# Cross attention: the value projection of an encoder chunk, taken apart from its key projection

## Chip, cores and metric

The kernel runs on one core of a Trainium2 chip. The metric is the device time of one execution in microseconds; the time before is the median of 7 runs. One further execution was profiled.

## What is computed

A post-norm decoder layer on `x` of 16 batches of 100 tokens, width 512: causal self-attention (16 heads of 32), cross attention to 361 encoder tokens per batch, and a mixture of 8 experts of which two are taken. Each of the three is added to its input and layer-normalised. The change lies in cross attention, in fp32:

```
q = rmsnorm((x @ Wq + bq) by 16 heads of 128) * qn_w
k = rmsnorm((enc @ Wk + bk) by 4 heads of 128) * kn_w     # each k, v head serves 4 q heads
v = (enc @ Wv + bv) by 4 heads of 128
out = softmax(q k^T / sqrt(128) + mask) v                 # per batch and head: 100 x 361 scores
x = layernorm(x + out @ Wo)
```

## The kernel before

**Products in three parts.** An fp32 operand is split into a high and a low half: `split` copies the high half (L137, mostly on ScalarE, a CAST in the profile) and subtracts it (L140, on VectorE, or on GpSimd where the source is not in PSUM). `mm3` then issues three matmuls, high by high (L145), low by high (L146), high by low (L147). `mmk` does so for four blocks of 128 of the contraction, so a projection of one chunk of tokens is 12 matmuls of 512 columns.

**Stages.** Self-attention comes first, then the q projections of all tokens (`b_q`), then cross attention, then the output projection (`d_part`), routing, the experts and the last norm. Queries go to memory (`qd`) and come back per batch and head group; attention outputs go to memory (`od`) and come back per tile of 128 tokens.

**Cross attention by units.** A unit is one batch `b` and one group `g` of four query heads that share a key and value head, so there are 64 units, four to a batch. The 361 encoder tokens of a batch are cut into three chunks (`CH`: 128, 128 and 105). The loop over `order` does, in each unit:

- for the next batch: `fetch_ctx` and `split_ctx` (encoder tokens, turned, tile `cT`, two buffers for three chunks), `kv_project`, and `kv_turn` one unit later;
- `x_load` of the queries for the unit after the next (`qf`, L732), which are split into the weight buffers WH and WL;
- the steps of `("s0", "a-", "t0", "s1", "s2", "t1", "a0", "t2", "s3", "a1")`: `s` is `x_scores` of one head of the next unit, `t` is `x_turn` of one chunk of this unit, `a` is `x_attend` of one chunk, where `a-` is the last chunk of the unit before;
- in every third unit from the ninth on, one row of `Wo` (`load_row`: a load of 256 KB on the sync queue at L480, tile `f_wo`, then a split into WH and WL by ScalarE and GpSimd). There are 16 such rows.

`kv_project` makes the keys of a chunk (`pk`), adds the bias (`ks`, L697, VectorE), makes its values (`pv`) and splits them into a slot of WH and WL, and then takes the RMS norm of the keys: four sums of squares (`ksq`, L706, VectorE), `rms_scale` and `rsqrt` (`v_k`, then `a_k` and `y_k` on ScalarE, then `t_k` and `r_k` on VectorE), and a product on GpSimd (L717). `kv_turn` transposes the normed keys (`ptk`, L727) and splits them (`kT`).

`x_scores` makes scores `s` of 100 x 362, adds the mask and takes the extreme in one VectorE instruction (L746), the exponential with its sum on ScalarE (L757), a reciprocal (L758), and the scaling on GpSimd (L759). `x_turn` transposes the probabilities of a chunk, one transpose per head (`ptp`, L767), and splits them (`pT`). `x_attend` adds the chunk's product to `av`, and after the last chunk ScalarE writes `o` (L787), which is stored to `od` (L792).

**Who sets the order.** The program is written in the order above, and a scheduler with a timeline model of its own then orders each engine's instructions; so a projection may stand some units ahead of its place in the source. Some loads are kept in program order on the sync queue. PSUM has 8 banks, two for each of the tags `mm` (projections), `s`, `t` (transposes) and `av`; keys and values of all chunks share the two of `mm`. Engines run their instructions in the built order, each waiting on semaphores.

Of the kernel before, what the change touches and what calls it, by code (L numbers as in the profile page):

```python
# [17 lines left out]
B, S, D = 16, 100, 512  # L18
# [8 lines left out]
CH = [(0, 128), (128, 128), (256, SE - 256)]  # L27
# [35 lines left out]
def tile_decoder_layer(  # L63
# [42 lines left out]
    def bank(tag, shape, name):  # L106
        return ps[-1].tile(shape, FP, name=name, tag=tag)
# [4 lines left out]
    def pair(p, shape, name, tag=None, bufs=None):  # L112
        k = {} if bufs is None else {"bufs": bufs}
        tag = tag or name
        return Pair(
            p.tile(shape, FR, name=f"{name}_h", tag=f"{tag}_h", **k),
            p.tile(shape, FR, name=f"{name}_l", tag=f"{tag}_l", **k),
        )
# [14 lines left out]
    def split(dst, src, high=None, low=None):  # L133

        high, low = high or nc.scalar, low or nc.vector
        if high is nc.scalar:
            ins = nc.scalar.copy(dst.h, src)  # L137
        else:
            ins = high.tensor_copy(dst.h, src)  # L139
        low.tensor_tensor(dst.l, src, dst.h.bitcast(FP), ALU.subtract)  # L140
        return ins

    def mm3(out, a, b, start, stop):

        nc.tensor.matmul(out, a.h, b.h, start=start, stop=False)  # L145
        nc.tensor.matmul(out, a.h, b.l, start=False, stop=False)  # L146
        nc.tensor.matmul(out, a.l, b.h, start=False, stop=stop)  # L147

    def mmk(out, a, b, n=KC):
        for k in range(n):  # L150
            mm3(out, a(k), b(k), k == 0, k == n - 1)
# [31 lines left out]
    def rms_scale(ss, p, n, name, p_=None):  # L183
        v = (p_ or small).tile([128, n], FP, name=f"v_{name}", tag=f"rms_v{n}")
        nc.vector.tensor_scalar(v[:p], ss, 1.0 / HD2, EPS_RMS, ALU.mult, ALU.add)
        return rsqrt(v[:p], p, n, name, p_=p_)
# [9 lines left out]
    def slot_of(s):  # L196
        return Pair(WH[:, s], WL[:, s])
# [324 lines left out]
    for k in range(KC):  # L522
        i = 4 * NU - 8 + k
# [113 lines left out]
    CT = {}  # L637

    def fetch_ctx(b):
        CT[b] = kvp.tile([128, KC, SE], FP, name=f"cf_{b}", tag="cf")  # L640
        nc.sync.dma_start(CT[b], ctxT[b])

    def split_ctx(b, i):
        c0, n = CH[i]
        CT[b, i] = pair(kvp, [128, KC, 128], f"cT_{b}_{i}", tag="cT", bufs=2)
        split(CT[b, i][:, :, :n], CT[b][:, :, c0 : c0 + n], low=nc.gpsimd)
# [34 lines left out]
    VS, KS, QX = {}, {}, {}  # L681
    wk, wv = units["wk"], units["wv"]

    spare = [slot_of(s)[:, k] for s in (4, 5) for k in range(KC)]

    def kv_project(b, i):
        c0, n = CH[i]
        if i == 0:
            K[b] = pair(w2, [128, NKV, SP], f"kT_{b}", tag="kT")
            nc.gpsimd.memset(K[b].h[:, :, SE:].bitcast(FP), 0.0)  # L690
            nc.gpsimd.memset(K[b].l[:, :, SE:].bitcast(FP), 0.0)
        ct = CT.pop((b, i))
        m = b * len(CH) + i
        pk = bank("mm", [128, D], f"pk2_{b}_{i}")
        mmk(pk[:n], lambda k: ct[:, k, :n], lambda k: wk[:, k, :])
        ks = w0.tile([128, D], FP, name=f"ks_{b}_{i}", tag="ks")
        nc.vector.tensor_tensor(ks[:n], pk[:n], bk_bc[:n], ALU.add)  # L697
        pv = bank("mm", [128, D], f"pv2_{b}_{i}")
        mmk(pv[:n], lambda k: ct[:, k, :n], lambda k: wv[:, k, :])
        VS[b, i] = spare[m % 6]  # L700
        split(VS[b, i][:n], pv[:n])
        kr = ks[:n].rearrange("p (h d) -> p h d", d=HD2)
        ss = small.tile([128, NKV], FP, name=f"kss_{b}_{i}", tag="kss")
        sq = w0.tile([128, HD2], FP, name=f"ksq_{b}_{i}", tag="sq", bufs=1)
        for h in range(NKV):
            nc.vector.tensor_tensor_reduce(  # L706
                out=sq[:n],
                in0=kr[:, h, :],
                in1=kr[:, h, :],
                scale=1.0,  # L710
                scalar=0.0,
                op0=ALU.mult,
                op1=ALU.add,
                accum_out=ss[:n, h : h + 1],
            )
        rs = rms_scale(ss[:n], n, NKV, f"k_{b}_{i}")
        nc.gpsimd.tensor_tensor(  # L717
            kr, kr, rs[:n].unsqueeze(2).to_broadcast([n, NKV, HD2]), ALU.mult
        )
        KS[b, i] = kr  # L720

    def kv_turn(b, i):
        c0, n = CH[i]
        kr = KS.pop((b, i))
        pt = bank("t", [128, NKV, 128], f"ptk_{b}_{i}")
        for h in range(NKV):
            nc.tensor.transpose(pt[:, h, :n], kr[:, h, :], ident[:n, :n])  # L727
        split(K[b][:, :, c0 : c0 + n], pt[:, :, :n])

    def x_load(b, g):  # L730
        qf = w0.tile([128, GR, S], FP, name=f"qf_{b}_{g}", tag="qf")
        nc.sync.dma_start(qf, qd[b][:, g * GR : (g + 1) * GR, :])  # L732
        QX[b, g] = spare[6 + g % 2][:, : GR * S].rearrange("p (h s) -> p h s", s=S)
        split(QX[b, g], qf, low=nc.gpsimd)
# [63 lines left out]
    for i in range(len(CH)):  # L798
        if i == 2:
            split_ctx(0, 2)  # L800
        kv_project(0, i)
        kv_turn(0, i)
    x_load(0, 1)
    for h in range(GR):
# [4 lines left out]
    def d_open():  # L809
        kv_l.close()  # L810
        inp["d"] = pool(d_i, "d_in", 2)
# [5 lines left out]
    def d_load(i):  # L817
        t, g = parts[i]
        n = TT[t][1]
        p = inp["d"]  # L820
        of = p.tile([128, GR, 128], FP, name=f"of_{t}_{g}", tag="of")
        nc.sync.dma_start(of[:, :, :n], od[t][:, g * GR : (g + 1) * GR, :n])
        OT[t, g] = pair(p, [128, GR, 128], f"ot_{t}_{g}", tag="ot")
        split(OT[t, g][:, :, :n], of[:, :, :n], low=nc.vector if i % 2 else nc.gpsimd)

    def d_part(i, among={}):

        t, g = parts[i]
        n = TT[t][1]
        if g == 0:  # L830

            tag = "av" if t == NT - 1 else "s" if t in (3, 4) else "mm"
            X1[t] = bank(tag, [128, D], f"acc_{t}")
        o, w = OT.pop((t, g)), units[f"wo_{g}"]
        for h in range(GR):
            mm3(
                X1[t][:n],
                o[:, h, :n],
                w[:, h, :],
                g == h == 0,  # L840
                g == NKV - 1 and h == GR - 1,
            )
            if h in among:
                among[h]()

    def d_norm(t):
        t0, n = TT[t]
        acc = X1.pop(t)
        p = w3 if t >= HEAD else inp["d"]
        x2 = p.tile([128, D], FP, name=f"x1_{t}", tag="x1", bufs=1 if t < HEAD else 3)  # L850
        nc.sync.dma_start(x2[:n], x1d[t][:n])
        nc.vector.tensor_tensor(x2[:n], acc[:n], x2[:n], ALU.add)
        layernorm(x2[:n], x2[:n], n, f"ln2_{t}")
        nc.sync.dma_start(x2d[t0 : t0 + n, :], x2[:n])
        X2[t] = x2
# [6 lines left out]
    for i, (b, g) in enumerate(order):  # L862
        if b == B - 1:
            if g == 0:
                d_open()
                d_load(0)
            for j in range(HEAD * g, HEAD * (g + 1)):
                d_load(j + 1)
                d_part(j)
                if parts[j][1] == NKV - 1:  # L870
                    d_norm(parts[j][0])
        if b + 1 < B:
            if g == 0:
                fetch_ctx(b + 1)
                split_ctx(b + 1, 0)
            if g < len(CH):
                kv_project(b + 1, g)
            if g + 1 < len(CH):
                split_ctx(b + 1, g + 1)
        if i + 2 < len(order):  # L880
            x_load(*order[i + 2])
        if b + 1 < B and g == NKV - 1:
            kv_turn(b + 1, 2)
        if b + 1 < B and 1 <= g < NKV - 1:
            kv_turn(b + 1, g - 1)
        nxt = order[i + 1] if i + 1 < len(order) else None
        for what in ("s0", "a-", "t0", "s1", "s2", "t1", "a0", "t2", "s3", "a1"):
            if what[0] == "s":
                if nxt:
                    x_scores(*nxt, int(what[1]))  # L890
            elif what[0] == "t":
                x_turn(b, g, int(what[1]))
            elif what[1] != "-":
                x_attend(b, g, int(what[1]))
            elif i:
                x_attend(*order[i - 1], 2)
        if i % 3 == 2 and 8 <= i < 8 + 3 * NKV * KC:
            w, k = divmod((i - 8) // 3, KC)
            load_row(f"wo_{w}", wo_slot[w], Wo4[w], k)
# [451 lines left out]
    for i in range(HEAD * NKV, len(parts)):  # L1351
        t, g = parts[i]
# [477 lines left out]
```

## Time and profile before

| what | value |
|---|---|
| median of 7 runs | 1409.3 us (1406.37 to 1413.98) |
| profiled execution | 1411.19 us |
| its span, first to last instruction | 1409.4 us |
| mean granted TensorE clock | 0.976 |
| cross attention, from the first scores to the last value projection | about 440 to 990 us |
| TensorE, VectorE, ScalarE, GpSimd busy (share of the span) | 95%, 67%, 54%, 50% |

In the profile PE is TensorE's matmuls, PEld its weight loads, DVE VectorE, ACT ScalarE, POOL GpSimd, SP or SPq the queue that issues most DMAs. A row of a timeline gives the start and the duration in us, the engine, the source line, the operation, the tile written and the tiles read, shapes, a count, and in brackets the idle time before it with what ended it. Matmuls are pipelined: one starts before the one before it has ended, so distances between starts are what counts. A mean granted clock under 1 means that the throttle held TensorE at half speed for stretches.

### The profile page before, as it was taken

The numbers are of one execution on the slowest core, as the hardware profiler recorded it, in microseconds if no ns is written. First come the engines' busy times: TensorE is split into PE (matmuls) and PEld (weight loads), VectorE is DVE, ScalarE is ACT, GpSimd is POOL, SyncE is SP. The second block draws the span as 40 slices with busy tenths as digits, with TensorE's granted clock in tenths as the row PEclk, the third lists the DMA queues.
The fourth block names the chain that finished last, engine by engine and source line by source line (L and its number), as shares of the span: only waits on it lengthen the run. The fifth ranks groups of instructions, "written<-read, shape, count | busy, mean of one in ns | idle before, by whom it ended". The sixth has DMA issues, their size and how long they took to land.

```text
span 1409.4 us, 25131 instructions
## 1 busy us (share of the span) xinstructions
PE 1337.6 (95%) x7952; PEld 1109.6 (79%) x7952; DVE 939.6 (67%) x2932; ACT 757.4 (54%) x1899; POOL 711.7 (50%) x839
## 2 busy tenths in 40 slices
PE   8999989999999999999999999999999898899895
PEld 7888868888878888888888888888887675677773
DVE  5766576766467777777777667767653558854577
ACT  4666653444446666666666656656663233333356
POOL 6877663344245555556555545555455345542530
PEclk9999999999999999999999999999999899899997
DMA  5221244645442122333233222322436545667883
GB/s 160 73 94 49 63 146 127 144 91 117 101 94 71 43 70 71 74 80 71 70 76 76 65 56 64 76 70 49 123 97 189 170 166 165 185 223 255 255 250 118
DMA packets 197872, 159.79 MB, mean 113 GB/s; under 512 B 133322, under 2 KB 152878, under 8 KB 197742
## 3 DMA queue, kind: packets, MB, share of 16 engines
q1 hardware_dynamic: 187904, 137.83, 35.8%
q0 software_dynamic: 4576, 14.95, 3.4%
q10 hardware_dynamic: 5262, 5.41, 1.3%
q8 instruction: 65, 1.06, 0.3%
q14 instruction: 65, 0.53, 0.1%
HBM read 107.16 MB, written 50.99 MB: 112 GB/s over the span
## 4 chain that ended last, share of the span: by engine, by line
PE 71%; DVE 13%; DMA 7%; ACT 4%; issue 3%; SPq 1%; POOL 1%; ACTq 0%; DVEq 0%; POOLq 0%
PE pq L145 4%; PE pq L147 4%; PE pq L146 4%; PE pv L145 4%; PE pv L146 4%; PE pv L147 4%; PE ptp L767 3%; PE pk L145 3%; PE pk L147 3%; PE pk L146 3%; PE s L145 3%; PE s L147 3%; PE s L146 3%; PE av L146 2%; DMA f_e<-in_expert_w 2%
## 5 line engine op out<-in xcount | busy, mean ns | idle before, releaser
L759 POOL TENSOR_SCALAR p<-p,sums 100x361 f32<-100x361 f32 x256 | 146.5, 577 | 101.5 <-DVE sums L758 90.5
L746 DVE CUSTOM_DVE_ANT_0 p<-s,nmask 100x361 f32<-100x361 f32 x256 | 133.0, 527 | 63.5 <-PE s L147 54.7
L757 ACT ACTIVATE p<-p,nm 100x361 f32<-100x361 f32 x256 | 153.2, 601 | 40.3 <-DVE nm L746 37.0
L140 DVE TENSOR_TENSOR pT_l<-ptp,pT_h 128x400 fp32r<-128x400 f32 (+1 forms) x192 | 107.5, 567 | 56.0 <-ACT pT_h L137 55.5
L145 PE MATMUL pq<-WH 128*128 128x512 f32 (+2 forms) x272 | 106.7, 392 | 5.5 <-DVE WH L139 5.5
L767 PE MATMUL ptp<-ident,p 100*128 100x100 f32 (+1 forms) x768 | 107.6, 252 | 0.0
L137 ACT CAST pT_h<-ptp 128x400 fp32r<-128x400 f32 (+1 forms) x192 | 91.2, 487 | 29.9 <-PE ptp L767 29.5
L140 POOL TENSOR_TENSOR cT_l<-cf,cT_h 128x512 fp32r<-128x512 f32 (+1 forms) x48 | 54.3, 1133 | 103.3 <-ACT cT_h L137 101.3
L767 PEld LDWEIGHTS ptp<-ident,p 100*128 100x128 f32 (+1 forms) x768 | 95.7, 152 | 13.4 <-POOL p L759 2.3
L146 PE MATMUL pq<-WL,WH 128*128 128x512 f32 (+2 forms) x272 | 104.0, 382 | 0.0
L147 PE MATMUL pq<-WH,WL 128*128 128x512 f32 (+2 forms) x272 | 103.8, 382 | 0.0
L147 PE MATMUL acc<-WH,ot_l 128*128 128x512 f32 (+1 forms) x208 | 86.6, 417 | 7.8 <-DVE ot_l L140 6.2
L145 PE MATMUL acc<-WH,ot_h 128*128 128x512 f32 (+1 forms) x208 | 86.2, 415 | 5.5 <-ACT ot_h L137 5.5
L145 PE MATMUL s<-kT_h,WH 128*100 128x362 f32 x256 | 88.2, 355 | 0.6 <-ACT kT_h L137 0.6
L145 PE MATMUL av<-pT_h,WH 128*128 128x400 f32 (+1 forms) x192 | 76.7, 400 | 8.5 <-ACT pT_h L137 8.1
L146 PE MATMUL acc<-WL,ot_h 128*128 128x512 f32 (+1 forms) x208 | 84.7, 407 | 0.0
L147 PE MATMUL s<-kT_h,WL 128*100 128x362 f32 x256 | 84.5, 330 | 0.0
L146 PE MATMUL s<-kT_l,WH 128*100 128x362 f32 x256 | 83.9, 328 | 0.0
L614 POOL TENSOR_TENSOR qs<-qs,r_q 128x512 f32<-128x512 f32 (+1 forms) x52 | 54.0, 1068 | 58.3 <-DVE r_q L169 47.9
L140 POOL TENSOR_TENSOR WL<-qf,WH 128x400 fp32r<-128x400 f32 x64 | 67.3, 1053 | 30.1 <-ACT WH L137 26.5
L145 PE MATMUL pv<-WH,cT_h 128*128 128x512 f32 (+1 forms) x192 | 79.2, 412 | 0.9 <-DVE WL L140 0.9
L145 PE MATMUL pk<-WH,cT_h 128*128 128x512 f32 (+1 forms) x192 | 77.6, 404 | 0.2
(337 smaller groups left out, 4010.2 us busy)
## 6 DMA issues: line engine op xcount, KB each, us to landing
qf<-qd SPq DMA_DIRECT2D x64, 200.0 KB
of<-od SPq DMA_DIRECT2D x48, 256.0 KB
cf<-in_ctxT SPq DMA_DIRECT2D x16, 722.0 KB
eb<-in_expert_b SPq DMA_DIRECT2D x32, 256.0 KB
ysd<-h SPq DMA_DIRECT2D x32, 256.0 KB
f_e<-in_expert_w SPq DMA_DIRECT2D x30, 256.0 KB
f_wq<-in_Wq SPq DMA_DIRECT2D x16, 256.0 KB
f_wo<-in_Wo SPq DMA_DIRECT2D x16, 256.0 KB
```

What stands on the lines that cost most here:

```text
L137: ins = nc.scalar.copy(dst.h, src)
L140: low.tensor_tensor(dst.l, src, dst.h.bitcast(FP), ALU.subtract)
L145: nc.tensor.matmul(out, a.h, b.h, start=start, stop=False)
L146: nc.tensor.matmul(out, a.h, b.l, start=False, stop=False)
L147: nc.tensor.matmul(out, a.l, b.h, start=False, stop=stop)
L614: nc.gpsimd.tensor_tensor(qr[:, hs, :], qr[:, hs, :], rs[:n, hs].unsqueeze(2).to_broadcast([n, GR, HD2]), ALU.mult,)
L746: nc.vector.tensor_tensor_reduce(out=p, in0=sc[:, :SE], in1=nmask, scale=1.0, scalar=BIG, op0=ALU.add, op1=ALU.min, accum_out=nm,)
L757: nc.scalar.activation(p, p, AF.Exp, bias=nm, scale=-1.0, accum_out=sh)
L759: nc.gpsimd.tensor_scalar(p, p, sh, 1.0, ALU.mult, ALU.mult)
L767: nc.tensor.transpose(pt[:n, h, :], probs[h][:, c0 : c0 + n], ident[:S, :S])
```

## The change

`kv_project` is cut into `k_project` and `v_project`. The bodies are the same lines; the values of a chunk are no longer made between the bias and the norm of its keys. In the first batch both are called in turn. In the loop, a unit's keys stay where they were (units 0, 1 and 2), and the values of the three chunks are made in units 0, 2 and 3. So a unit has 24, 12, 24 and 12 projection matmuls where it had 24, 24, 24 and none, counted in the source. A chunk's encoder tokens (`CT[b, i]`) are now released by `v_project`.

```diff
-    def kv_project(b, i):
+    def k_project(b, i):
         c0, n = CH[i]
...
-        ct = CT.pop((b, i))
-        m = b * len(CH) + i
+        ct = CT[b, i]
         pk = bank("mm", [128, D], f"pk2_{b}_{i}")
         mmk(pk[:n], lambda k: ct[:, k, :n], lambda k: wk[:, k, :])
         ks = w0.tile([128, D], FP, name=f"ks_{b}_{i}", tag="ks")
         nc.vector.tensor_tensor(ks[:n], pk[:n], bk_bc[:n], ALU.add)
-        pv = bank("mm", [128, D], f"pv2_{b}_{i}")
-        mmk(pv[:n], lambda k: ct[:, k, :n], lambda k: wv[:, k, :])
-        VS[b, i] = spare[m % 6]
-        split(VS[b, i][:n], pv[:n])
         kr = ks[:n].rearrange("p (h d) -> p h d", d=HD2)
...
         KS[b, i] = kr
+
+    def v_project(b, i):
+        n = CH[i][1]
+        ct = CT.pop((b, i))
+        pv = bank("mm", [128, D], f"pv2_{b}_{i}")
+        mmk(pv[:n], lambda k: ct[:, k, :n], lambda k: wv[:, k, :])
+        VS[b, i] = spare[(b * len(CH) + i) % 6]
+        split(VS[b, i][:n], pv[:n])
...
-        kv_project(0, i)
+        k_project(0, i)
+        v_project(0, i)
...
             if g < len(CH):
-                kv_project(b + 1, g)
+                k_project(b + 1, g)
+            for j in ((0,), (), (1,), (2,))[g]:
+                v_project(b + 1, j)
             if g + 1 < len(CH):
                 split_ctx(b + 1, g + 1)
```

## The prediction

> **What bounds the kernel now.** I read four things in this order: the page, the stage table cut into one encoder batch per row, the list of waits of TensorE for 400 to 990 us, and then timelines of single batches.
>
> ```profile
> span 1409.4 us, 25131 instructions
> PE 1337.6 (95%) x7952; PEld 1109.6 (79%) x7952; DVE 939.6 (67%) x2932; ACT 757.4 (54%) x1899; POOL 711.7 (50%) x839
> ...
> PE 71%; DVE 13%; DMA 7%; ACT 4%; issue 3%; SPq 1%; POOL 1%; ACTq 0%; DVEq 0%; POOLq 0%
> ```
>
> TensorE is busy 95% of the span and carries 71% of the chain that ended last. The change lies between about 434 and 990 us, so I ask how full TensorE is there. Two neighbouring batches, cut from one group of key sums to the next:
>
> ```profile
> 572.20:611.60 39.40, 38.75 (x218) 32.73 (x217) 28.80 (x110) 25.74 (x71) 22.44 (x31) 1.00 0.31 69
> 611.60:649.70 38.10, 37.86 (x217) 32.31 (x217) 27.71 (x110) 25.03 (x69) 21.03 (x30) 1.00 0.31 81
> ```
>
> After the window and its length come TensorE, weight loads, VectorE, ScalarE and GpSimd, each busy us and instructions, then the granted clock. A batch takes 38.1 to 39.4 us, of which TensorE is busy all but 0.2 to 0.7. No other engine passes 29. So there is no empty fourth unit: the scheduler already runs the projections some units ahead of their place in the source. Only waits can be won or lost, and the waits of TensorE name them:
>
> ```profile
> PE av L145 <- ACT pT_h L137: 8.1, 10, 1.7
> PE av L146 <- DVE pT_l L140: 4.2, 20, 0.5
> PE pv L145 <- DVE WL L140: 0.9, 1, 0.9
> PE s L145 <- ACT kT_h L137: 0.6, 2, 0.3
> ```
>
> Each row gives the sum, the count and the longest. Together they are 13.8 us in 15 batches, nearly all on turned probabilities (pT). Most of the 8.1 us has a DMA behind it. ScalarE works in order, and a cast of a Wo row stands in its queue before the row has landed:
>
> ```profile
> 629.01 0.59 ACT L787 ACTIVATE o<-av,bvT 128x400 f32<-128x400 f32 x1 [2.03 <-PE av L147]
> ...
> 632.94 0.64 ACT L137 CAST cT_h<-cf 128x512 fp32r<-128x512 f32 x1
> 634.78 0.62 ACT L137 CAST WH<-f_wo 128x512 fp32r<-128x512 f32 x1 [1.20 <-DMA f_wo<-in_Wo]
> 635.31 0.58 ACT L137 CAST WH<-pv 105x512 fp32r<-105x512 f32 x1
> ```
>
> The sync queue issues the row's load only after the store of o (L792 before L480), so the cast can start 634.78 - 629.01 = 5.8 us after o starts, whatever else happens. All 16 Wo rows wait like this, 24.6 us of ScalarE in sum. Whether TensorE pays depends on what stands behind the cast.
>
> **The change part by part.** Both programs have the same instructions (each TensorE, VectorE, ScalarE and GpSimd count is equal), so nothing is saved by itself; only order and buffers move. The sync queue's order is the same up to the last batch but for one swapped query load. From the built orders, one steady batch reads, with k1, k2, v1, v2 for the 12 products of a key or value chunk of the next batch, k0', v0' for the batch after, s for the three products of a head's scores, t for single transposes:
>
> before: ... [v1] ... [k2] s, t, s, t t, v2 in three pieces with t t between them, s, s, 6 products, ..., [k0'] ...
> after: ... [k2] ... [v1] s, t, s, six t, s, [v2] s, 1, s, 2, ..., [k0'] ...
>
> So k2 and v1 change places, and v2 goes whole behind the transposes. I price each place by distances in TensorE's row against the chain that must end in between. Steps of TensorE: 0.23 us per projection product, 0.16 to 0.18 per score or attend product, 0.09 per transpose.
>
> ```profile
> 513.86 0.40 PE L147 MATMUL pv<-WH,cT_l 128*105 128x512 f32 x1
> 514.09 0.40 PE L145 MATMUL pv<-WH,cT_h 128*105 128x512 f32 x1
> 514.33 0.34 PE L767 MATMUL ptp<-ident,p 100*128 100x100 f32 x2
> 514.44 0.46 PE L146 MATMUL pv<-WL,cT_h 128*105 128x512 f32 x1
> 514.74 0.39 PE L147 MATMUL pv<-WH,cT_l 128*105 128x512 f32 x1
> ```
>
> 1. v2 in one piece: after a pair of transposes the next product but one starts 0.30 us on (514.44 to 514.74) where 0.23 is usual (513.86 to 514.09). Two such breaks fewer in a batch, 14 batches: 2 x 0.07 x 14 = -2.0; new breaks of v0' and of head products by scores give some back. I take -1.4, between -2.6 and 0.
>
> 2. PSUM bank of v1 and v2. In the built program k2's bank is held until the ks evacuation (which waits for the k0 transposes, as before), so v2 takes v1's bank and waits for both splits of v1 (CAST WH, then TENSOR_TENSOR WL). Count from the start of v1's last product. ScalarE: cT_h of the next batch at 0.2 (it waits for v1, its buffer's last reader), WH at 0.7 to 1.3. VectorE first has the masked minimum of the score product behind v1 (1.0 to 1.5, from 0.48 us wait and 0.54 duration at 511.87), then WL 0.69, to 2.2. Behind the waiting cT_h on ScalarE stand WH of v1, o of unit 3 and an exponential, none due sooner. TensorE has in between: 0.23 + 0.5 + 0.36 + 0.09 + 0.5 + 0.53 + 0.5 = 2.7. Slack 0.5, price 0. The cover is those scores and transposes; without it 1 us per batch would show.
>
> 3. k0' behind v2 (it takes v2's bank). TensorE reaches it at 8.8 on the same count: 2.7, then 2.8 for v2, then s, 1, s, 2, four t, 3, the four key transposes, s: 0.5 + 0.18 + 0.5 + 0.36 + 0.36 + 0.55 + 0.4 + 0.5 = 3.3. Without a Wo row WL of v2 ends at 7.4: free. With one: in the new ScalarE order the row of Wo that is loaded after o of unit 3 stands ahead of cT_h and WH of v2 (before: the order is mixed, and k0' comes later behind v2). o starts at 1.3 at best, behind cT_h and WH of v1. The row lands at 1.3 + 5.8 = 7.1; casts at 7.1, 7.6, 8.1 (0.53 apart, as at 634.78 and 635.31), WH ends 8.7, WL 9.5. TensorE waits 0.7 in 4 batches (the rows return every third batch): 2.8.
>
> 4. The Wo row loaded after o of unit 0 (4 batches). Before, o stood ahead of the root of the key norm (a_k, y_k) on ScalarE; now behind a_k, a query cast and y_k, which wait for VectorE's sums:
>
> ```profile
> 601.54 0.60 ACT L787 ACTIVATE o<-av,bvT 128x400 f32<-128x400 f32 x1 [1.19 <-PE av L147]
> 602.03 0.20 ACT L157 ACTIVATE a_k<-v_k 105x4 f32<-105x4 f32 x1
> ...
> 607.40 0.62 ACT L137 CAST WH<-f_wo 128x512 fp32r<-128x512 f32 x1 [1.63 <-DMA f_wo<-in_Wo]
> ...
> 608.38 0.49 ACT L137 CAST pT_h<-ptp 105x400 fp32r<-105x400 f32 x1
> ```
>
> Walking VectorE's new order on from term 3 (WL, minimum, pT_l, ks, minimum, four key sums with kT_l among them) ends v_k at 12.2; a_k, cast and y_k then let o start at 13.3, which is 4.5 after k0'. Before it was 601.54 - 597.99 = 3.55. So the row lands 0.9 later, and the cast of the third chunk of pT stands behind it. TensorE, which comes 0.2 us later than before, waits 0.25 for pT_h and 0.46 for pT_l; it waited 0.25 to 0.4 before. Net 0.4 x 4 = 1.6.
>
> Walks 3 and 4 start every operation at once. Where the trace has such a tight run (second chunk of unit 2, at 536 us) the products came another 0.37 and 0.43 late. So I do not take the bare 0.7 and 0.4 but 0.9 and 0.8: 3.6 and 3.2. Ends: 0 (the load lands sooner) and 1.3 and 1.7 (o a little later), that is 0 to 12.
>
> Here a rule is weighed. "DMA: Bandwidth & Descriptors", section on the anatomy of one DMA, fits 2.0 us plus bytes by 436 GB/s for one DMA issued by GpSimd, a path that no run here times. That makes an estimate of 2.6 us for 256 KB, against 4.7 us from issue to cast here (630.05 to 634.78). By the rule both rows would have landed before ScalarE asks for them, and terms 3 and 4 would be nil. The rows of this kernel, 16 of 16 waited for, speak otherwise, and the sum goes by them.
>
> 5. Unit 2 (pT_l of the second chunk, 0.4 to 0.5 in nearly every batch) has the same instructions in the same order on TensorE, VectorE and ScalarE before and after: 0.
>
> 6. The last batch and the experts behind it: the scheduler also shuffles products of the output projection and, late, the turn and product of one expert slice. After 985 us TensorE is busy 378 of 425 us by the stage table, so order can matter there in both directions, and no row prices this one: 0, from -5 to +5.
>
> Sum: -1.4 + 3.6 + 3.2 = +5.4. The profiled execution took 1411.2 us (span 1409.4 and 1.8 around it), 1.9 above the median 1409.3. So 1416.6 for a like execution, 1414.7 against the median. About 0.3%, 4.2 us, is what a measurement of this kernel can tell from no change; the forecast is a little above it.
>
> **The rivals.** *Same* (0.30): the new waits are paid back. Whenever TensorE stands, ScalarE and VectorE catch up, and the 12.3 us of waits on pT (8.1 + 4.2) shrink by as much. For it: these waits are of the same kind. Against: they are short chains inside one unit that start from a TensorE product, so they do not profit from an earlier stop. Time 1409 to 1413. *Faster* (0.22): v1 behind k2 keeps its split out of VectorE's way before the reciprocals of heads 2 and 3 (sums at 509.71 stood behind WL at 509.11), everything behind it on VectorE comes 0.7 us sooner, and the waits on pT close. Half of them plus term 1 at its full size: -6 - 2 = -8, 1401. Against: TensorE did not wait at those reciprocals. *Much slower* (0.10, a part of slower): term 2's slack is lost. It needs WL of v1 0.5 us later, one exponential more on ScalarE; from there each 1 us is 14 us: 5.4 + 14 gives 1429. That the change doesn't do what it says is contained in the built order: it does not fill a fourth unit, since none was empty.
>
> **How the numbers follow.** Forecast (slower by over 0.3%, with the much slower part) 0.48, same 0.30, faster 0.22. The forecast's own range is 1413.5 (the bound) to 1425 (terms 3 and 4 at 12, term 6 at +5). The 8-in-10 range takes in the same case, most of the faster and stops short of the much slower: 1402 to 1426.
>
> **What would show it.** Right: on TensorE a wait of the first pk product on WL, 0.5 to 1.3 us in every third batch; ScalarE's o behind y_k; f_wo waits above 24.6 us; pv products 0.23 apart. Wrong: TensorE waiting on WL before every second value block (term 2), pT waits below 8 us in sum (faster), or a difference that lies behind 990 us.

## The result

The changed kernel took 1413.79 us (median of 20 runs), the kernel before 1408.86 us (48 runs on the same chip): 5 us more. The ratio of the means of these runs is 1.0040, 95% interval 1.0029 to 1.0051. It is slower by 0.4%, and the forecast of 1414.7 us was within a microsecond of the median. What the sum was made of held less well, and the experiments were needed to see that.

The profiled execution after is a quick one of its kind (1409.87 us, clock 0.979), so its span says nothing about the change; its waits do. From the page:

```profile
span 1408.1 us, 25110 instructions
PE 1329.5 (94%) x7952; PEld 1105.2 (78%) x7952; DVE 931.6 (66%) x2932; ACT 755.9 (54%) x1899; POOL 712.4 (51%) x839
...
PE 65%; DVE 12%; DMA 10%; ACT 5%; issue 4%; POOL 2%; SPq 1%; ACTq 1%; POOLq 0%; DVEq 0%
```

The counts are the same; the chain gives TensorE 65% where it had 71%, and DMA 10% where it had 7%. The two neighbouring batches:

```profile
570.60:609.20 38.60, 37.96 (x218) 32.65 (x217) 28.48 (x109) 25.19 (x70) 22.25 (x31) 1.00 0.33 77
609.20:648.00 38.80, 37.75 (x218) 32.62 (x217) 28.26 (x111) 24.98 (x70) 21.15 (x30) 1.00 0.25 63
```

Together 77.4 us against 77.5. The first is 0.8 us shorter than before; the second is 0.7 us longer, and it holds one of the new waits shown below (at 635.6 us, 0.72 us late). The waits of TensorE for 400 to 990 us (sum, count, longest):

```profile
PE av L145 <- ACT pT_h L137: 11.5, 20, 1.7
PE av L146 <- DVE pT_l L140: 3.0, 18, 0.2
PE pk L145 <- DVE WL L140: 1.6, 3, 0.7
PE pv L145 <- DVE WL L140: 0.9, 1, 0.9
```

They sum to 17.0 us, 3.2 more than before. New is the row of pk on WL, the wait that step 3 announced; a fourth one of 0.3 us shows only in the distances. And pT_h is waited for 20 times instead of 10. The first of the announced waits in the timeline:

```profile
512.16 0.52 SPq L480 DMA_DIRECT2D f_wo<-in_Wo  x1
...
516.31 0.62 ACT L137 CAST WH<-f_wo 128x512 fp32r<-128x512 f32 x1 [2.17 <-DMA f_wo<-in_Wo]
516.83 0.62 ACT L137 CAST cT_h<-cf 128x512 fp32r<-128x512 f32 x1
517.36 0.58 ACT L137 CAST WH<-pv 105x512 fp32r<-105x512 f32 x1
...
517.97 0.69 DVE L140 TENSOR_TENSOR WL<-pv,WH 105x512 fp32r<-105x512 f32 x1 [1.88 <-ACT WH L137]
...
518.71 0.50 PE L145 MATMUL pk<-WH,cT_h 128*128 128x512 f32 x1 [0.40 <-DVE WL L140]
```

ScalarE waits 2.17 us for the row, then come its cast, cT_h and WH of v2 in that order, then WL on VectorE, and only then k0'. TensorE's product before it started at 517.99, so k0' comes 0.73 us behind it where 0.16 is usual, 0.57 late; in the other three such batches it is 0.72, 0.31 and 0.83 late. That is 2.4 us in four batches.

The second new wait lies where the prediction had no price, in the experts:

```profile
1251.55 0.80 PE L1268 MATMUL gb<-is_in,opens 128*1 128x21 f16 x26
...
1253.22 1.03 POOL L1294 DMA_INDIRECT xs<-x2d,idx  x1 [6.71 <-DVE bat L1280]
...
1259.45 0.63 PE L1310 MATMUL pte<-ident,xs 128*128 128x128 f32 x4 [1.42 <-DMA xs<-x2d,idx]
1260.78 0.80 PE L1310 MATMUL pte<-ident,xs 128*128 128x128 f32 x4 [0.70 <-DMA xs<-x2d,idx]
```

The products `gb` make the second slot table (`slots`), from which GpSimd gathers the token rows of expert slice 11 (`xs`), which are then turned (`pte`). Before, the table stood at the turn of slice 9; in the new order it stands one slice later, at the turn of slice 10. Less work is left between the table and the turn of slice 11, and that turn and the next wait 2.1 us for gathered rows. The same place in the profile before, where one more slice (the turn at 1256.39 and its products) lies between and no turn waits for a gather:

```profile
1252.78 0.80 PE L1262 MATMUL gb<-is_in,opens 128*1 128x21 f16 x26
1254.76 0.95 POOL L1288 DMA_INDIRECT xs<-x2d,idx  x1 [6.20 <-DVE bat L1274]
1256.39 0.60 PE L1304 MATMUL pte<-ident,xs 128*128 128x128 f32 x4
1259.92 0.63 PE L1304 MATMUL pte<-ident,xs 128*128 128x128 f32 x4 [0.16 <-issue]
```

From the first turn to the last matmul the stage took, before and after (length first, granted clock third from last):

```profile
1212.70:1398.00 185.30, 166.90 (x811) 131.71 (x808) 115.33 (x354) 84.28 (x165) 60.65 (x63) 0.93 0.72 229
```

```profile
1206.80:1394.60 187.80, 167.52 (x811) 131.52 (x809) 114.20 (x350) 83.70 (x164) 61.47 (x64) 0.93 0.71 224
```

2.5 us more at the same clock, with the same 811 matmuls.

### The profile page after: what moved, and what is told of

Same layout as the page of the kernel before. It is cut to its first block, busy times and chain, and to the rows that moved or that the text cites. A ratio compares the mean times of both kernels' runs of the same rounds, so it can differ in the third digit from the quotient of the medians.

```text
span 1408.1 us, 25110 instructions
## 1 busy us (share of the span) xinstructions
PE 1329.5 (94%) x7952; PEld 1105.2 (78%) x7952; DVE 931.6 (66%) x2932; ACT 755.9 (54%) x1899; POOL 712.4 (51%) x839
## 4 chain that ended last, share of the span: by engine, by line
PE 65%; DVE 12%; DMA 10%; ACT 5%; issue 4%; POOL 2%; SPq 1%; ACTq 1%; POOLq 0%; DVEq 0%
PE pq L145 4%; PE pq L147 4%; PE pq L146 4%; PE pv L145 4%; PE pv L146 3%; PE pv L147 3%; DMA f_wo<-in_Wo 3%; PE pk L145 3%; PE ptp L770 3%; PE pk L147 3%; PE pk L146 3%; PE s L145 2%; PE s L146 2%; PE s L147 2%; DMA f_e<-in_expert_w 2%
## 5 line engine op out<-in xcount | busy, mean ns | idle before, releaser
L770 PE MATMUL ptp<-ident,p 100*128 100x100 f32 (+1 forms) x768 | 102.1, 251 | 0.0
L770 PEld LDWEIGHTS ptp<-ident,p 100*128 100x128 f32 (+1 forms) x768 | 92.3, 151 | 7.3
L712 POOL TENSOR_TENSOR ks<-ks,r_k 128x512 f32<-128x512 f32 (+1 forms) x48 | 50.0, 1041 | 91.5 <-DVE r_k L169 79.8
L145 PE MATMUL pv<-WH,cT_h 128*128 128x512 f32 (+1 forms) x192 | 77.4, 403 | 1.0 <-DVE WL L140 0.9
```

What stands on the lines that cost most here:

```text
L712: nc.gpsimd.tensor_tensor(kr, kr, rs[:n].unsqueeze(2).to_broadcast([n, NKV, HD2]), ALU.mult)
L770: nc.tensor.transpose(pt[:n, h, :], probs[h][:, c0 : c0 + n], ident[:S, :S])
```

## The experiments

The theories are those of the expectations: A, the Wo row ahead of the split of v2; U, the later turned probabilities of unit 2; B, the experts' order; C, more time at half clock. The runs were made on three chips (e1 to e4, e5 to e8, e9 to e12), where the kernel before took 1420, 1423 and 1416 us; every ratio is to the kernel before on the same chip. Each run also gives its span and mean granted clock. The records show the clock only whole or halved, so span x (1 - clock) is the time withheld, an upper bound of what the throttle cost (stretches in which TensorE waits at half clock count too); the rest is called the net span. Differences of both to the kernel before are means over the runs, with one standard error.

| run | median, before | ratio (95%) | net span, us | withheld, us |
|---|---|---|---|---|
| e1 only row batches | 1423.1, 1420.2 | 1.0034 (1.0012 to 1.0055) | +5.5 ± 1.0 | -1.6 ± 1.0 |
| e2 all but row batches | 1424.0, 1420.2 | 1.0028 (1.0007 to 1.0050) | +0.4 ± 1.0 | +3.6 ± 1.0 |
| e3 after, row early | 1430.6, 1420.2 | 1.0079 (1.0049 to 1.0109) | +7.8 ± 1.0 | +2.8 ± 1.2 |
| e4 before, row early | 1423.1, 1420.2 | 1.0016 (0.9996 to 1.0036) | +1.8 ± 1.2 | -0.1 ± 1.1 |
| e5 before, rows behind unit 3 | 1404.4, 1422.5 | 0.9887 (0.9865 to 0.9909) | -13.3 ± 1.4 | -4.5 ± 1.3 |
| e6 after, rows behind unit 3 | 1418.5, 1422.5 | 0.9987 (0.9968 to 1.0005) | -1.2 ± 0.9 | -1.5 ± 1.2 |
| e7 after, rows behind unit 0 | 1414.5, 1422.5 | 0.9948 (0.9930 to 0.9966) | -4.9 ± 1.1 | -2.6 ± 0.9 |
| e8 after, table early | 1426.0, 1422.5 | 1.0036 (1.0015 to 1.0057) | +0.2 ± 0.6 | +3.7 ± 1.3 |
| e9 after again | 1422.2, 1416.0 | 1.0046 (1.0027 to 1.0065) | +3.1 ± 0.8 | +3.4 ± 0.8 |
| e10 four rows moved | 1421.8, 1416.0 | 1.0040 (1.0019 to 1.0061) | +0.7 ± 1.0 | +4.9 ± 0.8 |
| e11 both removed | 1417.3, 1416.0 | 1.0007 (0.9988 to 1.0027) | +1.3 ± 0.8 | +0.2 ± 0.8 |
| e12 split only | 1418.7, 1416.0 | 1.0009 (0.9987 to 1.0031) | +0.1 ± 0.9 | +1.6 ± 1.0 |

**What of the change moves anything (e12).**

```diff
-            for j in ((0,), (), (1,), (2,))[g]:
+            for j in ((0,), (1,), (2,), ())[g]:
```

> Only the function is cut in two: the values of chunk i are made in unit i as before, behind the norm of the chunk's keys. The built order is that of the kernel before on every engine, so this tells what the comparison makes of no change, and that the cut by itself costs nothing: ratio 1.000, within 0.002.

1.0009, no change: the cut of the function costs nothing. The orders of the built programs tell the rest. With only v2 moved to unit 3 the order is still that of before on every engine; with only v1 moved to unit 2 it is that of the changed kernel. So the whole change is one key block and one value block that change places, and what follows from it.

**The change in halves (e1, e2).** In e1 the new places hold only for the four batches whose v2 meets a row, in e2 everywhere but there:

```diff
+            late = b + 1 in (3, 6, 9, 12)        # e2: not in
-            for j in ((0,), (), (1,), (2,))[g]:
+            for j in (((0,), (), (1,), (2,)) if late else ((0,), (1,), (2,), ()))[g]:
```

> The changed order only where the values of batches 3, 6, 9 and 12 are made, the four batches in which the row of Wo loaded after o of unit 3 meets the first key block of the next batch; elsewhere, in the last batch and in the experts the order is that of the kernel before. The whole change cost a ratio of 1.0040, about 5.6 us. Theory A, the Wo row (term 3): the four waits of the first pk product on WL (0.3 to 0.8 us each in the profile after, 2.4 us in sum, 2.8 with the next product) stay and most of the cost stays: ratio 1.002 to 1.004. Theory U, unit 2 (pT of the second chunk, which comes some 0.27 us later in every batch of the profile after): 4 of 14 batches, +1 us, ratio 1.0007. Theory B, the experts' order (the stage from the first expert product to the end was 2.5 us longer in the profile after, with half-clock windows taken out): 0, ratio 1.000. Theory C, no order at all but more half-clock windows: ratio anywhere, with the granted clock lower by 0.002 or more.

> The opposite half: the changed order everywhere but where the values of batches 3, 6, 9 and 12 are made; the last batch and the experts have the changed order but for one swap. Theory A (Wo row): no wait of the first pk product on WL, ratio 1.000 to 1.001. Theory U (unit 2): 10 of 14 batches, +2.7 us, ratio 1.002. Theory B (experts): all of it, expert stage again 2.5 us longer than before's, ratio 1.002 to 1.004. Theory C: as in the first run.

Both halves are slower, and in different ways. e1 has four waits of pk on WL, 3.4 us in its profile, no wait for xs, and its ratio is where theory A had it; the 5.5 us more net span are more than these waits. e2 has one wait of pk of 0.2 us and the wait for xs (2.2 us). Its ratio is where U and B had it, but it is made of 3.6 us more withheld clock and no more net span. That neither had foretold; C may have a part in it.

**Rows loaded a unit earlier (e3, e4), which did not do what they were for.** In e3 on the changed kernel, in e4 on the kernel before:

```diff
+        if i % 3 == 1 and 7 <= i < 7 + 3 * NKV * KC:
+            fetch_row(...)                       # row (i - 7) // 3
         if i % 3 == 2 and 8 <= i < 8 + 3 * NKV * KC:
-            load_row(...)
+            split_row(...)                       # row (i - 8) // 3
```

> The changed kernel with each Wo row loaded one unit (about 9 us) before its split instead of just ahead of it. Theory A: ScalarE's waits for f_wo go from 31.6 us to under 3 us, the waits of pk on WL go to 0, and the time comes back to that of before, ratio 0.998 to 1.000. Theory U: rows explain nothing, ratio 1.003. Theory B: expert stage as in the changed kernel, ratio 1.002 to 1.004. Theory C: as the clock falls.

> The kernel before with each Wo row loaded one unit before its split. Tells what the late rows cost in the old order: ScalarE's 24.6 us of waits for f_wo go. If pT's third chunk behind a row costs TensorE what its waits show (1.2, 1.5, 1.9 and 0.7 us behind the rows after unit 1, 1.5 and 1.6 behind those after unit 2), the ratio is 0.995 to 0.998; if these waits are paid back elsewhere it is 1.000. The expert order is that of before but for one swap.

The waits of ScalarE for the rows should have gone. In e3 they are

```profile
ACT WH L137 <- DMA f_wo<-in_Wo: 40.4, 16, 3.2
```

and in e4 30.3 us, 16 of 16. The scheduler moved the cast forward with the load (why is not shown), so each row stood in ScalarE's queue as unready as before, only at another place (pk on WL in e3: 4 times, 4.3 us). This tells nothing against A; why e3 lost as much as 0.8% is left open.

**Rows at one place per batch (e5, e6, e7).** The way to move a cast is to move what it stands behind:

```diff
+    ROWS = [*range(0, 64, 4)]                    # e5 and e6; e7: range(1, 62, 4)
-        if i % 3 == 2 and 8 <= i < 8 + 3 * NKV * KC:
-            w, k = divmod((i - 8) // 3, KC)
+        if i in ROWS:
+            w, k = divmod(ROWS.index(i), KC)
```

> The kernel before with all 16 Wo rows loaded after o of unit 3 (one in each batch, from the first) instead of after every third unit. In the profile before, TensorE waited 1.2, 1.5, 1.9 and 0.7 us for pT behind the rows loaded after o of unit 1, 1.5 and 1.6 us behind those after unit 2, 0.3 to 0.4 us three times behind those after unit 0, and not at all behind those after unit 3. The experts' order is that of before. Theory A (a Wo row costs TensorE what stands behind its cast): those 9 us go, ratio 0.993 to 0.996. Rival (such waits are paid back by fewer waits elsewhere, as in the run that loaded the rows a unit earlier): ratio 1.000.

> The changed kernel with the same placing of the rows: every batch has now the meeting of a Wo row and the split of v2 that term 3 of the prediction names, 14 or more instead of 4. Theory A: the first pk product waits for WL in nearly every batch, 0.3 to 1.3 us each, 9 to 14 us in sum, against 9 us saved behind the other rows; with the experts' later table (+2) ratio 1.001 to 1.005, and 0.4 to 0.8% above the next run. Rival (the meeting costs nothing lasting): equal to the next run.

> The changed kernel with all 16 rows loaded after o of unit 0, where no row meets the split of v2. Theory A: no wait of pk on WL; behind each row pT's third chunk waits 0.2 to 0.4 us as in the profile after, 3 to 6 us in sum, against 9 us and the 2.4 us of term 3 saved; with the experts' later table (+2) ratio 0.996 to 0.999. Rival: ratio 1.004 as the change itself.

Waits of TensorE for 400 to 990 us, e5:

```profile
PE av L145 <- ACT pT_h L137: 3.4, 7, 2.2
PE av L146 <- DVE pT_l L140: 2.4, 15, 0.2
PE pk L145 <- DVE WL L140: 0.3, 2, 0.2
```

e6:

```profile
PE pk L145 <- DVE WL L140: 12.3, 13, 1.7
PE av L145 <- ACT pT_h L137: 4.5, 14, 0.3
PE av L146 <- DVE pT_l L140: 2.8, 15, 0.6
```

e7, where pk waits for nothing:

```profile
PE av L145 <- ACT pT_h L137: 7.0, 19, 0.7
PE av L146 <- DVE pT_l L140: 4.0, 25, 0.2
```

With a row in every batch at the place that step 3 named, the wait of pk on WL comes 13 times for 12.3 us. With the same rows at the same place in the old order (e5) pk waits 0.3 us, and between e5 and e6 lie 14 us (0.9887 to 0.9987). From the first scores to the last value projection the three profiles hold no stretch at half clock (clock third from last; e5, e6, e7):

```profile
433.90:980.90 547.00, 541.84 (x3089) 464.20 (x3088) 399.26 (x1548) 356.69 (x970) 301.69 (x415) 1.00 0.30 69
432.70:993.80 561.10, 541.40 (x3093) 467.12 (x3092) 401.22 (x1553) 354.32 (x974) 301.44 (x415) 1.00 0.30 67
434.20:987.00 552.80, 541.27 (x3081) 465.47 (x3080) 400.57 (x1544) 357.73 (x975) 300.20 (x415) 1.00 0.29 67
```

TensorE is equally busy in all three, and the stage is 14.1 us longer in e6 than in e5, 12.0 of it in the waits of pk. That is the strongest evidence for A: one DMA wait, harmless or not by what is queued behind it. e7, where pT_h waits behind the rows up to 0.7 us each, is 0.39% or 5.5 us faster than e6 (0.9948 to 0.9987). e5 is 1.1% faster than the kernel before: the 8 to 9 us that pT waited behind rows are gone, and more than the expected 0.4 to 0.7%. So e6 and e7 also came out lower than theory A had them against the kernel before; the differences between the three are about what it foretold. Of the 18 us that e5 gained, 4.5 are clock given back, and some 4 to 5 of the net span are not accounted for.

**One dependency, one slice (e8), and the two causes on one chip (e9 to e11).** e8 puts the turn of slice 10 behind the table's last product (`placed`); e10 moves the four rows; e11 does both:

```diff
             ins = nc.tensor.transpose(pt[:, k, :], xs[:, k * 128 : (k + 1) * 128], ident)
+            if i == EARLY - 1:
+                in_turn(ins, placed[0])
...
+    ROWS = [i + (i % NKV == 0) for i in range(8, 56, 3)]
```

> The changed kernel with one dependency added: the turn of expert slice 10 stands behind the products of the second slot table (slots), so that the table comes one slice earlier, between the product of slice 9 and the turn of slice 10, nearly where the kernel before has it. Theory B (the scheduler put the table a slice later, so that the gather of slice 11 lands later and TensorE waits 2.1 us for xs, as in all three profiles with the changed order and in none with the old): that wait falls under 0.7 us, the expert stage is 1.5 to 2.5 us shorter, ratio 1.002 to 1.003. Rival (the table waits for its inputs there and costs the same): a wait of gb on is_in of 1 us or more, stage unchanged, ratio 1.004.

> The changed kernel once more, beside the three that follow on the same chip, since the kernel before took 1420 to 1423 us on the chips of the first eight runs and 1409 where the change was first timed. If the cost is made of waits that hang on when a load lands, it grows with them: ratio 1.004 to 1.007.

> The changed kernel with only the four Wo rows that meet the split of v2 moved one unit on (loaded after o of unit 0 instead of after o of unit 3); the other twelve rows and the experts' order stay. Theory A: the waits of pk on WL (2.4 to 4.3 us in sum) go, 0.2 to 0.4 us behind each moved row come, net 2 to 3 us off the changed kernel's time, ratio 0.0015 to 0.002 below it. Rival: the same as the changed kernel.

> The changed kernel with the four rows moved and the second slot table one slice earlier. If term 3 and the later table are the whole cost, the kernel is back at the time of before: ratio 0.999 to 1.001, and the expert stage is 1.5 to 3 us shorter than in the run before this one. If the longer waits of unit 2 cost what they show (0.27 us per batch more, 3.8 us), 1.002 to 1.003 stays.

The wait for xs is there in all seven profiles that have the new order of the table (1.9 to 2.2 us) and in those with the old order it is 0.4 us at most; e8 has 1.4 us, e11 none. In e10 and in e11 the stage reads:

```profile
1219.60:1404.30 184.70, 166.89 (x811) 132.67 (x809) 115.47 (x350) 83.62 (x164) 62.70 (x64) 0.92 0.72 228
```

```profile
1218.60:1401.20 182.60, 166.17 (x811) 132.50 (x809) 115.61 (x350) 83.42 (x163) 63.24 (x64) 0.92 0.74 231
```

2.1 us less for the table one slice earlier, at one clock. The other profiles agree. With the time at half clock counted half, by the clock records of the traces, the stage takes 171.7 and 171.6 us with the new order (e2, e3) and 169.7 and 170.1 with the old (e1, e4) on their chip; 173.6 and 173.4 with the new (e6, e7), 170.7 with the old (e5) and 170.6 with the early table (e8); 170.9 and 169.3 with the new (e9, e10), 169.5 with the old (e12) and 167.2 with the early table (e11). So the later table costs its stage some 2 to 3 us, about the wait for xs.

The change itself came out again on this chip (e9, 1.0046). With both causes removed the kernel is back at the time of before (1.0007, and the null run e12 has 1.0009). One removal alone does not show in the time. Moving the four rows (e9 to e10) took 1.1 ± 1.4 us off the mean, where theory A had 2 to 3; the net span fell by 2.5 ± 1.2 us, while 1.5 ± 0.9 us more clock were withheld. e8, with the table early and the rows in place, stayed at 1.0036, above the 1.002 to 1.003 expected, with a wait for xs of 1.4 us (under 0.7 expected) and 3.7 us more withheld. Moving the table as well as the rows (e10 to e11) takes 4.0 ± 1.3 us off the mean, by the split 4.7 ± 0.9 us off the withheld time and nothing off the net span (+0.7 ± 1.2), though the stage's own row became shorter. So the split into net span and withheld time is not exact, and what the clock adds isn't settled; that the two removals together undo the change is.

e11 also speaks on theory U. It still waits 16.1 us for pT_h, 3.5 more than e12, which has the old order, on the same chip, and is as fast as e12 (0.3 ± 1.1 us less). The 1.002 to 1.003 that should have stayed if these waits cost what they show did not stay, though the interval of e11 (0.9988 to 1.0027) does not exclude the lower end.

## Why the prediction was right, and where it was not

**Step 3, the row ahead of v2's split: right.** Place, order of the queue, and count (four batches) were as told; the waits were 2.4 us in the profile after and 3.3 to 4.3 us in e1, e3, e8 and e9, against the 3.6 us of the sum. In time the four meetings are priced only roughly: 3.7 ± 1.2 us when only they are there (e1; 5.5 ± 1.0 of net span), 1.1 ± 1.4 us when they are taken away (e9 to e10; 2.5 ± 1.2 of net span). Here the weighed rule is decided too. By the Trainium skill's page "DMA: Bandwidth & Descriptors" (anatomy of one DMA) a row would land 2.6 us after its issue, an estimate. From issue to cast the trace after shows 4.15 us (512.16 to 516.31), the wait is there, and e6 shows it 13 times over. The page's fit is for GpSimd's path; this row on the sync queue took some 1.5 us longer.

**Step 4, the row behind o of unit 0: wrong, +3.2 that did not come.** The order was as told, o behind y_k:

```profile
600.57 0.20 ACT L158 ACTIVATE y_k<-a_k 105x4 f32<-105x4 f32 x1
600.68 0.59 ACT L790 ACTIVATE o<-av,bvT 128x400 f32<-128x400 f32 x1
...
606.61 0.62 ACT L137 CAST WH<-f_wo 128x512 fp32r<-128x512 f32 x1 [1.55 <-DMA f_wo<-in_Wo]
607.14 0.48 ACT L137 CAST pT_h<-ptp 105x400 fp32r<-105x400 f32 x1
...
607.89 0.35 PE L145 MATMUL av<-pT_h,WH 105*128 105x400 f32 x1
608.28 0.45 PE L146 MATMUL av<-pT_l,WH 105*128 105x400 f32 x1
```

But o starts 4.05 us after k0' (596.63), not 4.5, and pT_h has ended (607.62) when TensorE comes for it (607.89); only the product with pT_l is some 0.2 us late, and in the three other such batches neither is. A walk of eight steps was out by 0.45 us, and the wait it predicted was of that size.

**Step 6, everything behind the last batch: priced at 0, wrong by some 2 to 3 us.** Its bounds of -5 to +5 held what came. But "a difference that lies behind 990 us" was the prediction's own sign of being wrong, and it came in part: with the time at half clock counted half, cross attention takes 555.6 us in the profile before and 556.2 in the one after, while the experts' stage is 2.5 us longer. On the chip of e9 the pair is 560.6 (e12) and 563.0 (e9), and 1.4 us in the experts' stage. Single profiles can't price this finely: e10 and e11, with one order in cross attention, are 2.6 us apart there. The wait for xs stood in the built order to be read: the table one slice later, a gather of some 6 us behind it (1253.22 to 1259.45), and 5.7 us of products before the turn. The prediction named the shuffle and did not price it.

**Step 5, unit 2: wrong in the waits by some 3 us, not shown wrong in time.** The first product of the second chunk came 0.52 to 0.59 us late in 13 batches, where it had been 0.16 to 0.55 late (7.2 against 3.4 us); its second product lost 0.6 us less. The instructions and their order are the same, as the step said, but not the distances: TensorE arrives a little sooner, and pT_h still stands behind y_k on ScalarE, which waits for VectorE's sums. That would be step 1's 1.4 us given back as a wait, part of the mechanism of the rival *same*, argued from the two timelines. e11, with these waits and without their time, speaks for it.

**Step 1, v2 in one piece:** the products of v2 follow each other 0.23 us apart in the trace after, as told; no run measures the 1.4 us by itself.

**Step 2: right.** pv waited for WL once, 0.9 us, in both profiles: v2 in v1's bank brought no new wait.

**Not in the prediction at all: the clock.** In e9 3.4 ± 0.8 us more of the clock were withheld than from the kernel before, about half of the loss on that chip (e12, with the order of before, has 1.6 ± 1.0). A forecast of 0.3% cannot leave out a term of that size; the 13 half-clock stretches in the profile before were there to be weighed. Whether the clock had a part in the first result is not known: the clock of the kernel before is on record there for one execution only.

So the sum was right although a term of +3.2 did not come, because some 2 to 3 us came from the experts' stage, priced at 0, and on one chip about as much from the clock, not priced at all. The mechanism named first is shown; that the size agrees is in good part luck.

## What to carry to other kernels

A load that an engine waits for in order cost here what was queued behind it, not what it waited (e5 against e6). So look at what follows the waiting instruction, and move the load to where nothing urgent does: here that brought 1.1% (e5), where the change under study lost 0.4%. Loading sooner did not help where the scheduler moved the consumer with the load (e3, e4). And a change in one stage of a scheduled program can shuffle another: compare the built orders to the end, and price each transfer whose cover became shorter.

## What was not expected of the hardware

One program differs by up to 1% from chip to chip, or from one time to another, which these runs don't separate (medians of the kernel before 1408.9 us where the change was first timed, then 1420.2, 1422.5 and 1416.0), and the loads show it: from the issue of a Wo row to its cast the mean over 16 rows is 4.4 us in the profiles before and after, and 4.8 to 4.9 us in e1, e9 and e12. The net span of the changed kernel was 1377.7 us at first and 1385.1 us in e9. Batches are longer there by some 0.4 us each, and so is what TensorE waits: 12.6 us for pT_h in e12, which has the order of before, against 8.1 us. That the loads are the reason for the longer batches is likely, not shown.

The time withheld by the clock differs between programs that are nearly the same: 32.8 us in e11 and 37.5 us in e10 (12 runs each, ± 0.6), which differ by one dependency in the source and ran on one chip. That the order is the cause is not shown. The built orders are the same up to the turn of expert slice 10, at 1263 us; yet of the 6.5 us by which the time at half clock differs in the two profiles, 3.4 lie ahead of that turn.
